# Checks of a bound moved inside a two-layer graph-attention kernel: Gram matrices four at a time, output bias and weight sums later

## The chip, the cores and the metric

The kernel runs on one core of a Trainium2 chip. The metric is the device time of one execution in microseconds (us), and 3038.89 us is the median of three runs of the kernel before (3038.54 to 3039.82). The core has several engines that run side by side, each working through its own list of instructions in order: TensorE (PE in the profile, with its weight loads as PEld) multiplies matrices, VectorE (DVE) and ScalarE (ACT) do elementwise work, GpSimd (POOL) helps with some of it, and SyncE (SP) issues transfers. Results of TensorE land in PSUM, which is used here as eight banks; everything else lives in SBUF.

## The reference, cut to what matters

There are 64 graphs ("batches" here) of 256 nodes with 512 features, and one 256x256 adjacency matrix for all.

```python
# layer 0: one attention head whose scores are a sum of two node terms
h = relu(layernorm(x));  Wh = h @ W
logits = leaky_relu(e_src[:, None] + e_dst[None, :], 0.2)    # e = Wh . a_src, Wh . a_dst
x = x + softmax(where(adj == 0, -inf, logits)) @ Wh
# layer 1: eight heads of 64
h = relu(layernorm(x))
q, k, v = h @ Wq.T + bq, h @ Wk.T + bk, h @ Wv.T + bv
attn = softmax(where(adj == 0, -inf, q @ k.T / 8))           # per head
x = x + (attn @ v) @ Wo.T + bo
```

The kernel computes both softmaxes without taking a maximum out first. That is safe as long as the scores are bounded, and the bound follows from the weights. So the kernel also proves the bound on the chip: for each pair of heads of Wq and Wk it forms a Gram matrix (a 128x128 block of weights times itself, with the parts between the two heads masked away by `diag`), squares it twice, and compares the row sums of absolute values with a limit. It also compares the squared lengths of the vectors `wa` and of the query and key biases, and the sum of squares of Wv. All answers go into a table `ok`; its smallest value per row, `okm`, goes through a last 1x1 matmul (`pok`) into a `flag`. After the main program the flag is read, and a general version of the kernel would run if the bound weren't proven. With the weights at hand it doesn't run. Nothing in the main program waits for the flag.

## The kernel before

**Stages.** The work on a batch g is cut into generators, each of which emits some instructions and yields: `normalize0` (three steps: statistics, activation `h`, node products on DVE with `wa`), `weights0` (edge weights: exponentials on ACT, then maximum, mask and sum on DVE, giving `em` and `esum`), `aggregate0` (matmuls into `pu`, copied to `uT`, then the row sums), `transform0` (matmuls with W into `po`, and the residual read on DVE, L495), `normalize1` (statistics, then `nmr` and the activation `xn`), `transpose1` (transposes into `pt`, `hT`, and sums of its blocks by `combine`), `project_qk` and `project_v` (seven products each, in a form of Strassen's scheme that needs the combined weights of `combine_w`, L161 to L165), `attention` (scores `psc`, exponentials, masks on DVE, values `pav`, row sums), `scale` and `output`.

**Order.** TensorE, VectorE, ScalarE and SyncE run exactly in the order in which the Python code emits instructions: the order is written out by hand. The lists `first`, `second`, `period` and `last` at the end of `bounded()` name a stage and a batch offset; `step(stage, g)` runs one stage up to its next yield. Period i works on batch i in layer 1, on i+1 and i+2 in layer 0, and on the outputs of i-2. The first pass (i = 0) uses `first + second`, after a prologue written out line by line. A matmul that needs a VectorE result emitted just before it therefore waits for all of VectorE's earlier entries too, and everything behind it on TensorE waits with it.

**The side work.** The proof is one more generator, `constants()`. `aside()` runs it up to its next yield. In the kernel before it is called four times in the prologue and then after every step of the first pass, until it is used up. Each of the eight Gram matrices (two weights, four blocks) goes alone through three calls: Gram matmuls (L333) and masking on DVE (L335); first squaring (L338) and a copy on DVE (L340); second squaring (L343) and the absolute row sums on ACT (L345). Then come the table entries (L347 to L363), the squares of Wv in four steps (L372), the reductions (L377 to L382) and the last matmul (L385). The first call also computes the output bias: `bv` times Wo into `pbias` (L307), added to `bo` (L314). GpSimd adds that bias to x, at L519, right after the activation `xn`.

**Buffers.** PSUM tiles come from a pool of eight banks, `bank()`. The copies of the upper right weight quarter, which the combined weights overwrite, come into two buffers with the tag `b12`, which the bias rows (L357) use as well.

Of the kernel before, what the change touches and what calls it, by code (L numbers as in the profile page):

```python
# [9 lines left out]
F32 = mybir.dt.float32  # L10
I32 = mybir.dt.int32
AF = mybir.ActivationFunctionType
# [4 lines left out]
P = 128  # L17
# [11 lines left out]
def kernel(  # L29
# [102 lines left out]
    def bounded():  # L132
# [6 lines left out]
        def bank(shape, name):  # L139
            return ps_mm.tile(shape, F32, tag="mm", name=name)  # L140
# [15 lines left out]
        def quarter_of(src, i, j):  # L156
            return src[i * HD : (i + 1) * HD, j * HD : (j + 1) * HD].rearrange(
                "(c p) e -> p c e", p=P
            )
# [134 lines left out]
            combine_w(wq_sb)  # L294
            combine_w(wk_sb)

        def constants():


            def whole(wt, src, nm):  # L300
                b12 = work.tile([P, DC // 2, HD], F32, tag="b12", name=f"b12_{nm}", bufs=2)
                nc.gpsimd.dma_start(b12, quarter_of(src, 0, 1))
                return ((wt[:, B11], b12), (wt[:, B21], wt[:, B22]))

            pb = bank([P, D], "pbias")
            for c in range(DC):
                nc.tensor.matmul(  # L307
                    pb,
                    cols["bv"][:, c : c + 1].to_broadcast([P, P]),
                    wo_sb[:, c, :],  # L310
                    start=(c == 0),
                    stop=(c == DC - 1),
                )
            nc.vector.tensor_add(bo_b, pb, bo_b)  # L314
            yield

            ok = weights.tile([P, 2 * DC + 5], F32, tag="ok", name="ok")  # L320
            diag = weights.tile([P, P], F32, tag="diag", name="diag")
            nc.vector.memset(diag, 0.0)
            nc.vector.memset(diag[0:DH, 0:DH], 1.0)
            nc.vector.memset(diag[DH:P, DH:P], 1.0)
            rows = weights.tile([P, 2 * DC], F32, tag="rows", name="rows")
            for j in range(2 * DC):
                e = j % DC
                if e == 0:
                    w_q = whole((wq_sb, wk_sb)[j // DC], (wqT, wkT)[j // DC], "qk"[j // DC])
                pg = bank([P, P], f"pgram_{j}")  # L330
                for c in range(DC):
                    wc = w_q[c // 2][e // 2][:, c % 2, (e % 2) * P : (e % 2 + 1) * P]
                    nc.tensor.matmul(pg, wc, wc, start=(c == 0), stop=(c == DC - 1))  # L333
                gm = work.tile([P, P], F32, tag="gram", name=f"gram_{j}", bufs=2)
                nc.vector.tensor_mul(gm, pg, diag)  # L335
                yield
                pg = bank([P, P], f"pgram2_{j}")
                nc.tensor.matmul(pg, gm, gm, start=True, stop=True)  # L338
                gm = work.tile([P, P], F32, tag="gram", name=f"gram2_{j}", bufs=2)
                nc.vector.tensor_copy(gm, pg)  # L340
                yield
                pg = bank([P, P], f"pgram4_{j}")
                nc.tensor.matmul(pg, gm, gm, start=True, stop=True)  # L343
                ab = work.tile([P, P], F32, tag="gabs", name=f"gabs_{j}")
                nc.scalar.activation(ab, pg, AF.Abs, accum_out=rows[:, j : j + 1])  # L345
                yield
            nc.vector.tensor_scalar(ok[:, 0 : 2 * DC], rows, 0.66, None, op0=ALU.is_le)  # L347
            junk = work.tile([P, D], F32, tag="junk", name="junk_b")
            sq = weights.tile([P, 4], F32, tag="sq", name="sq")
            nc.vector.memset(sq, 0.0)  # L350
            for j in range(2):
                nc.vector.scalar_tensor_tensor(
                    junk, wa[j], 1.0, wa[j], op0=ALU.mult, op1=ALU.mult, accum_out=sq[:, j : j + 1]
                )
            for j, src in enumerate((bq, bk)):
                row = work.tile([1, D], F32, tag="b12", name=f"brow_{j}", bufs=2)
                nc.gpsimd.dma_start(row, src.rearrange("(o e) -> o e", o=1))  # L357
                nc.vector.scalar_tensor_tensor(
                    junk[0:1, :], row, 1.0, row, op0=ALU.mult, op1=ALU.mult,
                    accum_out=sq[0:1, 2 + j : 3 + j],  # L360
                )
            nc.vector.tensor_scalar(ok[:, 2 * DC : 2 * DC + 2], sq[:, 0:2], 1.95, None, op0=ALU.is_le)
            nc.vector.tensor_scalar(ok[:, 2 * DC + 2 : 2 * DC + 4], sq[:, 2:4], 1.0, None, op0=ALU.is_le)  # L363
            yield
            big_v = weights.tile([P, 1], F32, tag="big_v", name="big_v")
            wv_q = whole(wv_sb, wvT, "v")
            svs = weights.tile([P, 2 * DC], F32, tag="svs", name="svs")
            for c in range(DC):
                for j in range(2):
                    sqv = work.tile([P, HD], F32, tag="junk", name=f"sqv_{c}_{j}")  # L370
                    wc = wv_q[c // 2][j][:, c % 2, :]
                    nc.vector.scalar_tensor_tensor(  # L372
                        sqv, wc, 1.0, wc, op0=ALU.mult, op1=ALU.mult,
                        accum_out=svs[:, 2 * c + j : 2 * c + j + 1],
                    )
                yield
            nc.vector.tensor_reduce(big_v, svs, AX.X, ALU.add)  # L377
            nc.vector.tensor_scalar(
                ok[:, 2 * DC + 4 : 2 * DC + 5], big_v, 1.0e8, None, op0=ALU.is_le
            )  # L380
            okm = weights.tile([P, 1], F32, tag="okm", name="okm")
            nc.vector.tensor_reduce(okm, ok, AX.X, ALU.min)  # L382
            yield
            pk = bank([1, 1], "pok")
            nc.tensor.matmul(pk, okm, ones[:, 0:1], start=True, stop=True)  # L385
            nc.vector.tensor_scalar(flag, pk, P - 0.5, None, op0=ALU.is_lt)
# [113 lines left out]
        def normalize1(g):  # L500
            xt = xts[g]
            mv = small.tile([P, NT, 2], F32, tag="mv", name=f"mv1_{g}")
            for t in range(NT):
                token_stats(mv[:, t, :], xt[:, t, :], f"1_{g}_{t}", small)
                if t == 0:
                    yield
            rstd = inverse_std(mv, f"1_{g}", small)
            yield
            nmr = small.tile([P, NT], F32, tag="nmr1", name=f"nmr1_{g}")
            nc.vector.scalar_tensor_tensor(  # L510
                nmr, mv[:, :, 0], -1.0, rstd, op0=ALU.mult, op1=ALU.mult
            )
            norms[g] = big.tile([P, NT, D], F32, tag="xn", name=f"xn_{g}")
            for t in range(NT):
                nc.scalar.activation(  # L515
                    norms[g][:, t, :], xt[:, t, :], AF.Identity,
                    bias=nmr[:, t : t + 1], scale=rstd[:, t : t + 1],
                )
                nc.gpsimd.tensor_tensor(xt[:, t, :], xt[:, t, :], bo_b, op=ALU.add)  # L519
            yield  # L520

        def transpose1(g):
# [6 lines left out]
            for t in range(NT):  # L529
# [3 lines left out]
                nc.scalar.activation(hT[:, :, t * P : (t + 1) * P], pt, AF.Relu)  # L533
                yield
            lefts[g] = a, combine(a, ("hs", str(g)))
            yield

        def project_qk(g):
# [168 lines left out]
        def steps(*todo):  # L707
            for stage, g in todo:
                step(stage, g)
# [3 lines left out]
        def aside(n=1):  # L713
            for _ in range(n):
                next(side, END)
# [14 lines left out]
        steps((normalize0, 0), (normalize0, 0))  # L730
        node_weights()
        edge_mask()
        steps((normalize0, 0), (weights0, 0), (normalize0, 1), (weights0, 0))
        steps((aggregate0, 0), (aggregate0, 0))
        prepare_qk()
        steps((aggregate0, 0), (aggregate0, 0), (normalize0, 1), (transform0, 0), (transform0, 0))
        steps((normalize1, 0), (transform0, 0), (transform0, 0), (normalize1, 0))
        aside()
        step(normalize1, 0)
        aside(3)  # L740
        steps((transpose1, 0), (transpose1, 0), (transpose1, 0), (normalize0, 1))
        combine_w(wv_sb)
        first = [
            (load, 3), K, K, (weights0, 1), K, N0, K, (weights0, 1), N0, K, (aggregate0, 1),
            (aggregate0, 1), N0, K, (aggregate0, 1), (aggregate0, 1), W,
        ]
        for i in range(G + 2):
            for stage, ahead in last if i == G else period if i else first + second:
                step(stage, i + ahead if (stage, ahead) not in ((weights0, 1), (aggregate0, 1)) else 1)
                aside()  # L750
        assert next(side, END) is END
        for gen in running.values():
            assert next(gen, END) is END
# [206 lines left out]
```

## Time and profile before

| | |
|---|---|
| median time | 3038.89 us |
| span of the profiled run | 3038.1 us |
| TensorE busy | 2989.2 us, 98% |
| TensorE weight loads busy | 2185.8 us, 72% |
| VectorE busy | 2124.6 us, 70% |
| ScalarE busy | 940.7 us, 31% |
| GpSimd busy | 296.4 us, 10% |
| granted TensorE clock, mean | 0.996 |

"Busy" is the sum of the instructions' durations with overlaps counted once, so a busy TensorE can still be one that runs at half pace. A float32 matmul shows as two records ("passes") in the trace; four matmuls that build one 128x128 Gram matrix are eight passes. In a row of the timeline the first number is the start in us from the span's beginning, the second the duration of the merged group, and the brackets hold the idle time of that engine before it and what ended this idle time.

### The profile page before, as it was taken

Reading aid. Unit: us, or ns where it says so; the run is one execution under the profiler, and the core shown is the slowest. Engines: PE = TensorE matmul, PEld = TensorE weight load, DVE = VectorE, ACT = ScalarE, POOL = GpSimd, SP = SyncE. Lnnn points to the kernel's source line nnn. Section 1 sums busy time; section 2 is a strip of 40 time slices with the busy share of each in tenths; the row PEclk is TensorE's granted clock in tenths of the full one; section 3 lists DMA queues with packets and bytes.
Section 4 is the critical chain, followed back from the end, with each engine's and each line's share of the span. In section 5 each row is a group of like instructions: output and inputs, shape, how many; then the busy total and the mean of one; then the engine's idle time right before and its main releaser. Section 6 shows DMA issues by size and latency. Waiting matters only on the chain. (4 is left out here: it accounts for less than half of the span.)

```text
span 3038.1 us, 45803 instructions
## 1 busy us (share of the span) xinstructions
PE 2989.2 (98%) x18166; PEld 2185.8 (72%) x18166; DVE 2124.6 (70%) x4118; ACT 940.7 (31%) x2003; POOL 296.4 (10%) x279
## 2 busy tenths in 40 slices
PE   6999999999999999999999999999999999999998
PEld 4777777777777777777777777777777777777775
DVE  5767777677677677677776776776776777777764
ACT  2333333333233233333333332332332333333321
POOL 1101101001011011011011010110110110110100
PEclk9999999999999999999999999999999999999999
DMA  3112222122122122122121221221221221222213
GB/s 125 11 35 36 33 38 35 30 41 35 29 39 39 29 39 37 31 39 31 37 36 31 40 36 29 42 35 29 39 39 29 39 32 36 36 32 39 29 23 42
DMA packets 82062, 110.79 MB, mean 36 GB/s; under 512 B 11762, under 2 KB 47602, under 8 KB 81842
## 3 DMA queue, kind: packets, MB, share of 16 engines
q1 hardware_dynamic: 81122, 105.95, 21.8%
q8 instruction: 145, 2.38, 0.3%
q0 software_dynamic: 720, 1.85, 0.2%
q14 instruction: 75, 0.61, 0.1%
HBM read 40.64 MB, written 33.55 MB: 24 GB/s over the span
## 5 line engine op out<-in xcount | busy, mean ns | idle before, releaser
L478 PE MATMUL po<-wo_sb,aT 128*128 128x512 f32 x1024 | 483.0, 595 | 4.7 <-DVE aT L671 4.7
L478 PE MATMUL po<-w_sb,uT 128*128 128x512 f32 x1024 | 471.0, 593 | 0.0
L611 DVE TENSOR_TENSOR ex<-ex,maskT 128x512 f32<-128x512 f32 x512 | 396.1, 814 | 7.3 <-ACT ex L606 1.4
L221 PEld LDWEIGHTS pqk<-hs,wq_sb 128*128 128x128 f32 x2048 | 265.1, 193 | 89.4 <-issue 89.4
L106 POOL TENSOR_TENSOR rstd<-ve,minus_half 128x2 f32<-128x2 f32 x128 | 89.6, 700 | 2382.4 <-DVE ve L104 2382.4
L606 ACT ACTIVATE ex<-psc 128x512 f32<-128x512 f32 x512 | 264.4, 602 | 125.6 <-PE psc L598 125.6
L478 PEld LDWEIGHTS po<-w_sb,uT 128*128 128x128 f32 x1024 | 180.1, 191 | 154.0 <-issue 154.0
L221 PE MATMUL pqk<-hs,wk_sb 128*128 128x128 f32 x2048 | 272.1, 276 | 0.0
L221 PE MATMUL pqk<-hs,wq_sb 128*128 128x128 f32 x2048 | 271.7, 276 | 0.0
L478 PEld LDWEIGHTS po<-wo_sb,aT 128*128 128x128 f32 x1024 | 175.9, 192 | 132.6 <-issue 129.8
L495 DVE SCALAR_TENSOR_TENSOR x<-po,rs,x 128x512 f32<-128x512 f32 x128 | 96.1, 750 | 240.8 <-PE po L478 240.8
L598 PE MATMUL psc<-qk 64*128 64x256 f32 x2048 | 255.7, 389 | 0.0
L221 PEld LDWEIGHTS pqk<-hT,wq_sb 128*128 128x128 f32 x1536 | 196.1, 191 | 80.2 <-issue 59.3
L623 PE MATMUL pav<-ex,v 128*64 128x256 f32 x2048 | 250.9, 386 | 2.8 <-DVE ex L611 2.3
L212 PE MATMUL pv<-wv_sb,hs 128*128 128x256 f32 x1024 | 253.2, 380 | 0.0
L221 PEld LDWEIGHTS pqk<-hs,wk_sb 128*128 128x128 f32 x2048 | 251.0, 193 | 0.0
L453 PE MATMUL pu<-em,h 128*128 128x256 f32 x1024 | 245.0, 383 | 3.7 <-DVE em L438 3.7
L613 DVE TENSOR_TENSOR sm<-ex 128x512 f32<-128x512 f32 x256 | 235.9, 922 | 8.9
L403 ACT ACTIVATE h<-x,nmr,rstd 128x512 f32<-128x512 f32 x128 | 97.2, 806 | 467.6 <-DVE nmr L396 467.6
L598 PEld LDWEIGHTS psc<-qk 64*128 64x128 f32 x2048 | 187.3, 186 | 68.4 <-issue 26.2
L519 POOL TENSOR_TENSOR x<-x,bo_b 128x512 f32<-128x512 f32 x128 | 197.7, 1563 | 255.5 <-ACT xn L515 255.5
L631 ACT COPY aT<-pav 128x512 f32<-128x512 f32 x128 | 75.1, 587 | 472.4 <-PE pav L623 459.9
(147 smaller groups left out, 3932.2 us busy)
## 6 DMA issues: line engine op xcount, KB each, us to landing
x<-in_x_dram SPq DMA_DIRECT2D x64, 512.0 KB, 5.4
rb<-rc SPq DMA_DIRECT2D x512, 64.0 KB, 4.7
out_dram<-x SPq DMA_DIRECT2D x128, 256.0 KB, 2.0
w_sb<-in_L_gnn_W_dram SPq DMA_DIRECT2D x1, 1024.0 KB, 8.5
wq_sb<-in_L_gnn_Wq_dram SPq DMA_DIRECT2D x4, 256.0 KB, 16.1
wk_sb<-in_L_gnn_Wk_dram SPq DMA_DIRECT2D x4, 256.0 KB, 12.5
wo_sb<-in_L_gnn_Wo_dram SPq DMA_DIRECT2D x1, 1024.0 KB, 8.5
wv_sb<-in_L_gnn_Wv_dram SPq DMA_DIRECT2D x4, 256.0 KB, 8.5
```

Source lines behind the costliest of these rows:

```text
L212: nc.tensor.matmul(dst[:, 0:HD], left[:, c, :], wt[:, slot, c, :], start=c == 0, stop=c == 1)
L221: nc.tensor.matmul(dst[:, at : at + P], wt[:, slot, c, e * P : (e + 1) * P], left[:, c, :], start=c == 0, stop=c == 1,)
L403: nc.scalar.activation(h[:, t, :], xt[:, t, :], AF.Relu, bias=nmr[:, t : t + 1], scale=rstd[:, t : t + 1])
L453: nc.tensor.matmul(pu[:, d, :], h[:, m, (dp + d) * P : (dp + d + 1) * P], em[:, m, :], start=(m == 0), stop=(m == NC - 1),)
L478: nc.tensor.matmul(dst, left(c, t), w_t[:, c, :], start=(c == 0), stop=(c == DC - 1))
L495: nc.vector.scalar_tensor_tensor(xt[:, t, :], po, rs[:, t : t + 1], xt[:, t, :], op0=ALU.mult, op1=ALU.add)
L519: nc.gpsimd.tensor_tensor(xt[:, t, :], xt[:, t, :], bo_b, op=ALU.add)
L598: nc.tensor.matmul(psc[r][:, m, :], qk[rows, 2 + e % 2, m * P : (m + 1) * P], qk[rows, e % 2, :], start=True, stop=True,)
L606: nc.scalar.activation(ex[:, r, :, :], psc[r], AF.Exp, scale=SCALE)
L611: nc.vector.tensor_mul(ex[:, r, :, :], ex[:, r, :, :], maskT)
L613: nc.vector.tensor_add(sm, ex[:, :, 0, :], ex[:, :, 1, :])
L623: nc.tensor.matmul(pav[r * DH : (r + 1) * DH, i, :], v[j][:, m, at : at + DH], pair[i][:, r, m, :], start=(m == 0), stop=(m == NC - 1),)
```

## The change

The change rearranges the proof and what stands beside it; what is computed stays the same.

- The Gram matrices go four at a time, one weight after the other, in six calls of `aside()`: 16 matmuls into four banks; four maskings on DVE; four squarings; four copies, now on ACT instead of DVE; four second squarings; four absolute row sums on ACT. A result is read one call after it was computed. The buffers for masked matrices grow from two to four.
- The first batch of four Gram matrices is emitted in the prologue after the first step of batch 0's `weights0`, where TensorE waits for that stage's second step. Its masking and first squaring follow batch 0's transform, the copies follow `normalize1`.
- In the first pass (i = 0) there is no further `aside()`. From period 1 on it is called after every second step.
- The output bias is a function of its own, emitted after those copies, and GpSimd's addition of it to x is emitted at the end of `transpose1` instead of in `normalize1`.
- The third step of batch 1's `normalize0` moves from the prologue to behind the first product of `project_qk`, and the combination of the value weights from the prologue to the beginning of `second`.

```diff
-        def constants():
+        def output_bias():
...
             nc.vector.tensor_add(bo_b, pb, bo_b)
-            yield
+
+        def constants():
...
-            for j in range(2 * DC):
-                e = j % DC
-                if e == 0:
-                    w_q = whole((wq_sb, wk_sb)[j // DC], (wqT, wkT)[j // DC], "qk"[j // DC])
-                pg = bank([P, P], f"pgram_{j}")
-                for c in range(DC):
-                    wc = w_q[c // 2][e // 2][:, c % 2, (e % 2) * P : (e % 2 + 1) * P]
-                    nc.tensor.matmul(pg, wc, wc, start=(c == 0), stop=(c == DC - 1))
-                gm = work.tile([P, P], F32, tag="gram", name=f"gram_{j}", bufs=2)
-                nc.vector.tensor_mul(gm, pg, diag)
-                yield
-                pg = bank([P, P], f"pgram2_{j}")
-                nc.tensor.matmul(pg, gm, gm, start=True, stop=True)
-                gm = work.tile([P, P], F32, tag="gram", name=f"gram2_{j}", bufs=2)
-                nc.vector.tensor_copy(gm, pg)
-                yield
-                pg = bank([P, P], f"pgram4_{j}")
-                nc.tensor.matmul(pg, gm, gm, start=True, stop=True)
-                ab = work.tile([P, P], F32, tag="gabs", name=f"gabs_{j}")
-                nc.scalar.activation(ab, pg, AF.Abs, accum_out=rows[:, j : j + 1])
-                yield
+            for n in range(2):
+                w_q = whole((wq_sb, wk_sb)[n], (wqT, wkT)[n], "qk"[n])
+                pgs = [bank([P, P], f"pgram_{n}_{e}") for e in range(DC)]
+                for e in range(DC):
+                    for c in range(DC):
+                        wc = w_q[c // 2][e // 2][:, c % 2, (e % 2) * P : (e % 2 + 1) * P]
+                        nc.tensor.matmul(pgs[e], wc, wc, start=(c == 0), stop=(c == DC - 1))
+                yield
+                gms = [
+                    work.tile([P, P], F32, tag="gram", name=f"gram_{n}_{e}", bufs=DC) for e in range(DC)
+                ]
+                for e in range(DC):
+                    nc.vector.tensor_mul(gms[e], pgs[e], diag)
+                yield
+                pgs = [bank([P, P], f"pgram2_{n}_{e}") for e in range(DC)]
+                for e in range(DC):
+                    nc.tensor.matmul(pgs[e], gms[e], gms[e], start=True, stop=True)
+                yield
...
+                for e in range(DC):
+                    nc.scalar.copy(gms[e], pgs[e])
+                yield
+                pgs = [bank([P, P], f"pgram4_{n}_{e}") for e in range(DC)]
+                for e in range(DC):
+                    nc.tensor.matmul(pgs[e], gms[e], gms[e], start=True, stop=True)
+                yield
+                for e in range(DC):
+                    j = n * DC + e
+                    ab = work.tile([P, P], F32, tag="gabs", name=f"gabs_{j}")
+                    nc.scalar.activation(ab, pgs[e], AF.Abs, accum_out=rows[:, j : j + 1])
                 yield
...
-                nc.gpsimd.tensor_tensor(xt[:, t, :], xt[:, t, :], bo_b, op=ALU.add)
...
             lefts[g] = a, combine(a, ("hs", str(g)))
+            for t in range(NT):
+                nc.gpsimd.tensor_tensor(xts[g][:, t, :], xts[g][:, t, :], bo_b, op=ALU.add)
             yield
...
-        steps((normalize0, 0), (weights0, 0), (normalize0, 1), (weights0, 0))
-        steps((aggregate0, 0), (aggregate0, 0))
+        steps((normalize0, 0), (weights0, 0))
+        aside()
+        steps((normalize0, 1), (weights0, 0), (aggregate0, 0), (aggregate0, 0))
         prepare_qk()
         steps((aggregate0, 0), (aggregate0, 0), (normalize0, 1), (transform0, 0), (transform0, 0))
         steps((normalize1, 0), (transform0, 0), (transform0, 0), (normalize1, 0))
+        aside(2)
+        step(normalize1, 0)
         aside()
-        step(normalize1, 0)
-        aside(3)
-        steps((transpose1, 0), (transpose1, 0), (transpose1, 0), (normalize0, 1))
-        combine_w(wv_sb)
+        output_bias()
+        steps((transpose1, 0), (transpose1, 0), (transpose1, 0))
         first = [
-            (load, 3), K, K, (weights0, 1), K, N0, K, (weights0, 1), N0, K, (aggregate0, 1),
-            (aggregate0, 1), N0, K, (aggregate0, 1), (aggregate0, 1), W,
+            (load, 3), K, (normalize0, 1), K, (weights0, 1), K, N0, K, (weights0, 1), N0, K,
+            (aggregate0, 1), (aggregate0, 1), N0, K, (aggregate0, 1), (aggregate0, 1), W,
         ]
         for i in range(G + 2):
-            for stage, ahead in last if i == G else period if i else first + second:
-                step(stage, i + ahead if (stage, ahead) not in ((weights0, 1), (aggregate0, 1)) else 1)
-                aside()
+            for n, (stage, ahead) in enumerate(last if i == G else period if i else first + second):
+                g = i + ahead
+                if i == 0 and ahead == 1 and stage in (normalize0, weights0, aggregate0):
+                    g = 1
+                if i == 0 and n == len(first):
+                    combine_w(wv_sb)
+                step(stage, g)
+                if i and n % 2:
+                    aside()
```

More of the change, by code (lines that the diff above doesn't have):

```diff
@@ L295, in prepare_qk @@
             combine_w(wk_sb)
-        def constants():
[L300 to L303, printed above, removed]
+        def output_bias():
             pb = bank([P, D], "pbias")
@@ L314, in constants, with whole @@
             nc.vector.tensor_add(bo_b, pb, bo_b)
-            yield
+        def constants():
+            def whole(wt, src, nm):
+                b12 = work.tile([P, DC // 2, HD], F32, tag="b12", name=f"b12_{nm}", bufs=2)
+                nc.gpsimd.dma_start(b12, quarter_of(src, 0, 1))
+                return ((wt[:, B11], b12), (wt[:, B21], wt[:, B22]))
             ok = weights.tile([P, 2 * DC + 5], F32, tag="ok", name="ok")
@@ new lines, in constants @@
+            for n in range(2):
[5 more added lines that the diff above has]
+                        nc.tensor.matmul(pgs[e], wc, wc, start=(c == 0), stop=(c == DC - 1))
+                yield
+                gms = [
[3 more added lines that the diff above has]
+                    nc.vector.tensor_mul(gms[e], pgs[e], diag)
+                yield
+                pgs = [bank([P, P], f"pgram2_{n}_{e}") for e in range(DC)]
+                for e in range(DC):
+                    nc.tensor.matmul(pgs[e], gms[e], gms[e], start=True, stop=True)
+                yield
+                gms = [
+                    work.tile([P, P], F32, tag="gram", name=f"gram2_{n}_{e}", bufs=DC)
+                    for e in range(DC)
+                ]
+                for e in range(DC):
[9 more added lines that the diff above has]
+                    nc.scalar.activation(ab, pgs[e], AF.Abs, accum_out=rows[:, j : j + 1])
```

## The prediction

> **What bounds the kernel now.** I read busy time by stretch first. Columns: stretch in us, its length, busy us and instruction count of TensorE (PE), its weight loads, VectorE (DVE), ScalarE (ACT) and GpSimd (POOL), granted clock, DMA share, GB/s.
>
> ```profile
> 0.00:45.90 45.90, 25.42 (x86) 16.08 (x87) 25.67 (x71) 11.24 (x19) 12.28 (x25) 1.00 0.63 206
> 45.90:92.70 46.80, 37.41 (x230) 31.55 (x228) 25.93 (x70) 10.37 (x34) 1.94 (x4) 0.89 0.00 1
> 92.70:115.60 22.90, 16.95 (x91) 13.73 (x90) 17.30 (x49) 6.23 (x11) 4.33 (x4) 0.85 0.05 13
> 115.60:154.90 39.30, 39.30 (x268) 30.75 (x266) 30.17 (x60) 14.61 (x31) 4.49 (x4) 1.00 0.22 28
> 200.00:3000.00 2800.00, 2799.48 (x17125) 2048.95 (x17122) 1981.19 (x3793) 880.42 (x1871) 268.83 (x239) 1.00 0.22 34
> ```
>
> From 115.6 us on PE never rests: 2799.48 of 2800 us. There a removed PE pass shortens the run by its whole length and an added one lengthens it. All slack lies in the first 115.6 us, where PE is busy 79.8 us and its clock is cut twice (0.89, 0.85). The cuts are 45.9 (first projection of batch 0), 92.7 and 115.6 (batch 0's two score steps); the fourth stretch is period 1 up to the same place for batch 1.
>
> Then the waits of PE up to 150 us (total, times, longest):
>
> ```profile
> PE pwa L268 <- DVE junk_a L261: 13.7, 4, 10.7
> PE pgram L338 <- DVE gram L335: 7.5, 5, 5.4
> PE pok L385 <- DVE okm L382: 5.9, 1, 5.9
> PE pu L453 <- DVE em L438: 3.7, 1, 3.7
> PE pgram L343 <- DVE gram L340: 2.6, 3, 1.5
> ```
>
> 16.0 us of these belong to the bound's proof (pgram, pok), which nothing else needs until the end. Last, PE in order of time (start, duration; in brackets idle before and releaser); the four parts are separate looks:
>
> ```profile
> 17.55 1.11 PE L280 MATMUL pmask<-ident,adj_f 128*128 128x128 f32 x4 [1.12 <-DVE adj_f L276]
> ...
> 37.61 3.60 PE L307 MATMUL pbias<-wo_sb,bv_c 128*128 128x512 f32 x8
> ...
> 53.24 0.79 PE L338 MATMUL pgram<-gram 128*128 128x128 f32 x2 [5.39 <-DVE gram L335]
> 53.83 1.91 PE L221 MATMUL pqk<-hs,wq_sb 128*128 128x128 f32 x8
> ...
> 100.69 0.19 PE L385 MATMUL pok<-ones,okm 128*1 128x1 f32 x2 [5.95 <-DVE okm L382]
> 100.85 2.05 PE L212 MATMUL pv<-wv_sb,hT 128*128 128x256 f32 x4
> ```
>
> A squaring at 53.24 holds PE 5.39 us, because its masked Gram matrix stands on DVE behind four node products (L410) and the values' combination (L162 to L165). The eight passes behind it take 1.91 us instead of the 1.06 at 45.90: each long idle is paid twice.
>
> **What the skill says.** The Trainium skill, "TensorE: Matmul & The Clock Gate", Part 1, states that the PE clock is halved after about 3.4 us idle and freed after about 3.4 us of work. The trace agrees: half pace after 5.39 and 5.95 us, full pace some 4 us later. The same page, on architectural detail, calls ACT and DVE strict first-in first-out; 53.24 shows what that costs. "SBUF — State Buffer", on SBUF's two sides, states that DVE and GpSimd share a port pair which one of them locks; here the masking product L611 takes 1.18 us each while the bias addition L519 runs (two in 2.36 at 143.83), and 0.64 without it (two in 1.29).
>
> **The change, part by part.** Pitches by the starts of following work: eight 128-wide passes 0.89 us (45.01 to 45.90), so a whole Gram matrix (four matmuls, shown as eight passes) 0.89 and a squaring 0.22; a 256-wide pass 0.21 (eight, 1.70); a 512-wide pass 0.43.
>
> (1) Four Gram matrices at 20.1. PE idles 3.68 us there, waiting for the edge weights, and the weights have landed: wq's quarters by about 20 (issued 2.3 to 4.0, 16.1 to landing), the fourth quarter at 16.9 (7.1+9.8). 32 passes cost 3.6 us at full pace and 7.1 at half. The four passes at 17.55 ran at half pace, so I take some 5.5, to 25.6. The aggregation then starts 1.8 later but warmer: its 16 passes took 6.5 us (23.78 to 30.30), against 3.4 at full pace. It ends between 28.5 and 31.
>
> (2) After the first transform (end T, 37.6 before) the order is: four maskings, four squarings, copies on ACT, then bias. DVE reaches the maskings at T+2.1, behind residual and statistics, and leaves at T+3.3; PE squares until T+3.4, bias until T+6.9, transposes until T+7.8. Projections start near T+8 (before: 45.90, T+8.3). Equal within 0.5; with (1), **-0.4**, from -2.2 to +1.
>
> (3) Projection to first scores. PE work left there: seven products of 16 passes 12.5, sixteen aggregation passes 3.4, sixteen transform passes 6.9, small ones 0.9: 23.7. DVE's queue gives new waits: node products end near K0+4.5 (PE wants them at 3.6), the edge weights near K0+11 (wanted at 9.9). The values' combination, 2.5 on DVE, now stands before the second half and delays only reads with free banks behind them. 23.7+0.7+1.1 = 25.5 instead of 46.8: **-21.3**. A cross-check: 15.3 idle and 5.3 of half pace (three stretches over twice their due) vanish over (3) and (4), and 79 proof passes (8.7) move out, 29.3 less new waits of 2.8.
>
> (4) First to second scores: the weight sums (eight of 0.46) with 1.67 us of DMA wait, and the 5.95 wait, leave. Period 1 does the same work in 14.7 (140.22 to 154.93); I add 1.0 for DVE's lag: 15.7 instead of 22.9: **-7.2**.
>
> (5) Period 1 receives one batch of four Grams (3.6), three batches of four squarings (2.6), and the last product (0.2): **+6.4**, undiminished since PE has no gap. Waits: the last squarings need copies behind the activation h on ACT, **+1.0** (0 to 2). While four banks are held, four turn over for the rest; I count nothing for that, at most 2. Then DVE. Batch 1's residual read frees DVE at 132.8. From there on the old clock it must do: ok, norms and bias rows 3.2 (89.88 to 93.08), weight sums 3.7, their transfer's rest 0.9 (landing 3.6 after the first bias row's read, less 2.7 of work), reductions 0.6, and its own statistics, residual, q/k read, reciprocal and edge weights, 6.6; ends at about 148. The final 1x1 matmul is emitted after the first values' product, which ends at 143.0: PE waits some **5.0** (1.4 if DVE has no lag, since edge weights end only at 143.9; 6 otherwise). Queued behind it are all the values' products. A wait over 3.4 brings half pace for some 3 us: **+1.5** (0 to 2). Sum +13.9.
>
> (6) The bias addition is emitted after the transposes. GpSimd's rows show it released by ACT's xn each time I looked (143.3 to 144.2, 189.5 to 190.4), and the change adds no operand, so it should start at the same moment; from period 2 on, nothing changes: 0.
>
> Sum: -0.4-21.3-7.2+13.9 = -15.0. **3038.9-15.0 = 3023.9 us.**
>
> **Rivals.** *The check is hidden* (25%): PE, slowed by 7 us in period 1, lets DVE catch up, and only the 1.4 remains. For: DVE idles 5.1 us between 130 and 140. Against: I count that idle already. 6.4+1.0+1.4 = 8.8; 3038.9-28.9+8.8 = 3018.8. *DVE becomes the bound* (8%): DVE works 43.2 us in the 69.7 of (3) and (4). Some 11 leave (maskings, copies, ok, weight sums), so 32 must fit into my 41.2. They should; but if DVE's order costs 14 us there, the gain is only that of (1) and a little: 3023.9+14 = 3038. *The repeated period suffers* (7%), the one on the slower side: the bias addition follows the transposes and its lock meets the combination (L170 to L173) and the maskings behind. At 0.3 us in each of 62 periods, 18.6: 3023.9+18.6 = 3042.5. Against: (6), and the period's PE has no DVE wait from 200 to 400 us that a small shift would lengthen. The forecast has 60%.
>
> **How the numbers follow.** Likeliest 3024. The first rival and the best ends of (1) and (5) reach 3014; the worst ends, with banks, reach 3033. Outside lie both bad rivals and a little more, under 2 in 10. Faster by over 0.2% (below 3032.8): 60+25 and 1 more, 0.86; within 0.2%: 0.07; slower: 0.07.
>
> **What would show it.** Right: Gram passes from 20.1; the first scores near 71 and the second near 87; busy PE from there except a wait of 3 to 6 us at the proof's last product, and some 6.4 us of pgram passes in period 1. Wrong: an aggregation that ends after 31; second scores after 95, which would make DVE the bound; period 1 with no wait (first rival) or with many bank waits; a period after 200 us longer than before.

## The result and the profile after

The changed kernel takes 3025.86 us (median of six runs, 3024.34 to 3028.91), beside 3039.36 us for the kernel before in the runs taken with it. The ratio is 0.9956, with a 95% interval from 0.9944 to 0.9969. The forecast was 3023.9 us, with a range from 3014 to 3033.

First the busy time by stretch, with the columns of the prediction's first fence. The cuts are at the same four places of the program: first projection of batch 0, its first and second score step, and the second score step of batch 1.

```profile
0.00:46.70 46.70, 28.48 (x106) 19.67 (x106) 26.06 (x72) 11.03 (x21) 10.52 (x25) 0.96 0.62 203
46.70:73.70 27.00, 24.61 (x152) 19.46 (x152) 20.73 (x47) 8.49 (x22) 3.18 (x3) 1.00 0.00 1
73.70:89.40 15.70, 14.99 (x90) 12.22 (x89) 13.40 (x25) 5.99 (x11) 3.60 (x3) 1.00 0.01 2
89.40:143.80 54.40, 48.91 (x326) 39.13 (x324) 37.12 (x96) 18.10 (x51) 5.66 (x6) 0.94 0.18 25
200.00:3000.00 2800.00, 2797.04 (x17111) 2045.73 (x17114) 1981.00 (x3789) 878.69 (x1867) 269.09 (x239) 1.00 0.22 35
```

The second stretch shrank from 46.8 to 27.0 us and lost its cut in the clock (0.89 before). The fourth grew from 39.3 to 54.4: TensorE executes 58 passes more there, idles 5.5 us, and runs at a mean clock of 0.94. In the last row TensorE is idle for 3.0 us instead of 0.5; the added 2.4 us lie after 2989 us, in the drain at the end of the run, which comes 11 us sooner and so begins before the fixed cut at 3000. In exact starts (first projection 46.76, scores 73.71, 89.40 and 143.83) the account is:

| Stretch | before | after | change | forecast |
|---|---|---|---|---|
| to the first projection | 45.90 | 46.76 | +0.9 | -0.4 |
| to the first scores | 46.85 | 26.95 | -19.9 | -21.3 |
| to the second scores | 22.87 | 15.69 | -7.2 | -7.2 |
| period 1 (to batch 1's second scores) | 39.31 | 54.43 | +15.1 | +13.9 |
| all the rest | 2883.2 | 2883.3 | +0.1 | 0 |

The sum is -11.0, the difference of the two profiled spans (3038.1 and 3027.1). The profiled execution of the changed kernel is the slowest of its six (3028.91); the medians differ by 13.5.

The waits of TensorE in the first 160 us:

```profile
PE pwa L268 <- DVE junk_a L261: 13.9, 4, 10.5
PE pok L400 <- DVE okm L397: 5.5, 1, 5.5
PE pgram L344 <- DVE gram L340: 2.3, 1, 2.3
PE pe L439 <- DVE junk L425: 1.3, 2, 0.8
PE pmask L280 <- DVE adj_f L276: 1.1, 1, 1.1
PE pu L468 <- DVE em L453: 1.0, 1, 1.0
PE pu L468 <- DVE s2v L197: 0.7, 1, 0.7
PE pqk L221 <- DVE hs L171: 0.7, 1, 0.7
```

The proof's waits fell from 16.0 us to 7.8, and what is left is two single waits. The last product's wait of 5.5 us is the old one (5.9) at a new place. TensorE in order of time around them, in three parts:

```profile
20.07 3.62 PE L334 MATMUL pgram<-wq_sb 128*128 128x128 f32 x16
...
26.31 3.62 PE L468 MATMUL pu<-em,h 128*128 128x256 f32 x16
...
39.52 2.05 PE L344 MATMUL pgram<-gram 128*128 128x128 f32 x8 [2.28 <-DVE gram L340]
41.36 4.28 PE L301 MATMUL pbias<-wo_sb,bv_c 128*128 128x512 f32 x8
...
122.31 1.13 PE L212 MATMUL pv<-wv_sb,hT 128*128 128x256 f32 x4
128.93 0.19 PE L400 MATMUL pok<-ones,okm 128*1 128x1 f32 x2 [5.49 <-DVE okm L397]
129.05 2.07 PE L212 MATMUL pv<-wv_sb,hs 128*128 128x256 f32 x4
```

At 20.07 the gap is gone: 32 Gram passes take 6.24 us, more than the 3.7 of the gap, but the 16 aggregation passes behind them take 3.45 instead of 6.5, so that the aggregation ends at 29.8, earlier than before (30.3). At 39.52 there is a new gap, 2.28 us of idle after the transform, the eight squaring passes take 1.84 us where 0.89 is due, and the bias passes behind it are slow (4.11 us from start to start of what follows, against 3.43 before). At 128.93 all of TensorE's work stands behind the last product, which waits for `okm`; the next group takes 1.87 us where 0.86 is due.

### The profile page after: what moved, and what is told of

Read it like the earlier page. It is cut to its first block, busy times and chain, and to the rows that moved or that the text cites. A ratio compares the mean times of both kernels' runs of the same rounds, so it can differ in the third digit from the quotient of the medians.

```text
span 3027.1 us, 45790 instructions
## 1 busy us (share of the span) xinstructions
PE 2987.1 (99%) x18166; PEld 2184.2 (72%) x18166; DVE 2124.1 (70%) x4110; ACT 941.3 (31%) x2011; POOL 296.5 (10%) x279
```

## The experiments

In each, the ratio is to the kernel before, run beside it on the same chip. The median of the kernel before is 3039.36 us beside the changed kernel, 3038.68 beside the next four experiments, 3038.05 beside the three after them and the one without a proof, and 3038.14 beside the two others. So a difference between two kernels of different groups is uncertain by about 1 us, and where it matters I read it in the traces too.

### The last product later

```diff
+            for _ in range(12):
+                yield
             pk = bank([1, 1], "pok")
```

> The changed kernel, with the proof's last 1x1 matmul and the flag emitted twelve calls later, so that it falls into period 2. Theory: the 5.5 us wait for okm and the half pace behind it (16 values' passes in 6.4 us instead of 3.4) leave, 8.8 us in all, and about 1.5 us come back as a wait of the aggregation for the edge weights, which VectorE finishes late: 3026 - 7 = 3019 us. Rival: VectorE's lateness is the real bound and the wait only moves to the next VectorE result: 3024 us or more.

Measured: 3019.33 us, ratio 0.9935 (0.9921 to 0.9948), 6.5 us below the changed kernel (5.9 if each is taken from the kernel before beside it). Period 1 takes 47.82 us (87.07 to 134.89) instead of 54.43, and the product finds its operand ready:

```profile
118.06 2.00 PE L616 MATMUL psc<-qk 64*128 64x256 f32 x16
131.40 0.66 PE L548 MATMUL pt<-ident,xn 128*128 128x128 f32 x4 [0.80 <-DVE s2v L197]
133.45 1.52 PE L641 MATMUL pav<-ex,v 128*64 128x256 f32 x12 [0.33 <-DVE v L206]
134.89 2.00 PE L616 MATMUL psc<-qk 64*128 64x256 f32 x16
144.02 0.19 PE L402 MATMUL pok<-ones,okm 128*1 128x1 f32 x2
```

So the wait was a cost of its own. VectorE's lag does come back, nearly in the size expected (1.1 us for 1.5), but as waits of 0.8 and 0.3 us for the values' sums rather than for the edge weights.

### The same move on the kernel before

The same lines with 24 in place of 12, and nothing else. Here a call comes after every step and there after every second one, so the distance in steps is the same.

> The kernel before with its last 1x1 matmul emitted 24 calls later, nothing else. Theory: VectorE carries the squares of the value weights ahead of the edge weights, so the aggregation waits for em at about 102.8 us where the matmul waited until 100.7; only part of the 5.95 us and the 2.1 us of half pace is won: 3035 to 3037 us. Rival, the matmul's wait is a cost of its own: 3039.4 - 8 = 3031 us.

Measured: 3035.56 us, ratio 0.9990 (0.9984 to 0.9997). Here the wait moved on:

```profile
91.86 2.00 PE L600 MATMUL psc<-qk 64*128 64x256 f32 x16
93.79 1.13 PE L212 MATMUL pv<-wv_sb,hT 128*128 128x256 f32 x4
...
96.48 1.89 PE L212 MATMUL pv<-wv_sb,hs 128*128 128x256 f32 x8
102.65 2.67 PE L455 MATMUL pu<-em,h 128*128 128x256 f32 x8 [4.28 <-DVE em L440]
```

The aggregation reaches the edge weights at 98.2 and gets them after 102.6. In the kernel before VectorE itself was late in this stretch; in the changed one, with the weight sums gone, the longest wait of the same stretch is 0.7. The theory holds: the move is worth 3.1 us alone (3038.68 less 3035.56), about half of what it is worth on top of the change.

### Two of the moves alone

```diff
-        steps((transpose1, 0), (transpose1, 0), (transpose1, 0), (normalize0, 1))
-        combine_w(wv_sb)
+        steps((transpose1, 0), (transpose1, 0), (transpose1, 0))
...
-            (load, 3), K, K, (weights0, 1), K, N0, K, (weights0, 1), N0, K, (aggregate0, 1),
+            (load, 3), K, (normalize0, 1), K, (weights0, 1), K, N0, K, (weights0, 1), N0, K, (aggregate0, 1),
...
+                if i == 0 and n == len(first):
+                    combine_w(wv_sb)
...
```

> The kernel before with two of the change's moves alone: batch 1's node products behind the first product, and the values' combination at the beginning of the second half. The proof stays one Gram matrix at a time in the first pass. Theory: the wait of 5.4 us at the first squaring and its 1.6 us of half pace leave, and 2.5 us of VectorE work come back in the second half, where VectorE is late: 3034 to 3036 us. Rival, the order of these two alone carries most of the gain: 3030 us or less. Second rival: VectorE bounds the first pass whatever the order: 3039 us.

Measured: 3031.91 us, ratio 0.9979 (0.9969 to 0.9988), about half of what the whole change gives, and 2 us better than my expectation. The wait of 5.4 us at the first squaring is gone (the longest at any squaring is now 1.0), and the first scores start at 84.18 instead of 92.75. The second half keeps its wait, now behind 2.2 us of VectorE waiting for the transfer of the value weights' quarter:

```profile
92.67 0.19 PE L385 MATMUL pok<-ones,okm 128*1 128x1 f32 x2 [6.49 <-DVE nmr L510]
```

The other half of the gain isn't taken apart. No run keeps one Gram matrix at a time and only starts the proof later, so it isn't shown what going four at a time, or copying on ScalarE, is worth by itself.

### The proof's first half not in the idle stretches

```diff
         steps((normalize0, 0), (weights0, 0))
-        aside()
...
-        aside(2)
         step(normalize1, 0)
-        aside()
         output_bias()
```

> The changed kernel with the first four Gram matrices, their masking, first squaring and copies moved out of the idle stretches ahead of the first pass; the whole proof now starts in period 1. Theory of the prediction, idle stretches hide them: period 1 gets 4.5 us of TensorE work more and the aggregation of batch 0 runs at half pace again, so 3026 + 5 = 3031 us. Rival, from the trace of the changed kernel: the squarings between transform and bias hold the projections back by about 4 us (2.3 idle, 1.8 of squarings, slow bias passes), so what is hidden at 20 us is paid there again: 3026 to 3027 us.

Measured: 3032.11 us, ratio 0.9978 (0.9968 to 0.9987). The number is the theory's, the reason isn't. The first scores start at 69.40, earlier than in the changed kernel (73.71) and than with the late product (71.38), which is the same program up to there. So the rival is right about the head of the run: what is saved at 20 us is lost again at 39. Period 1 takes 63.3 us, 8.8 more, of which 4.5 are work; the wait for `okm` grew to 10.3.

```profile
69.40 2.00 PE L614 MATMUL psc<-qk 64*128 64x256 f32 x16
...
140.97 0.19 PE L400 MATMUL pok<-ones,okm 128*1 128x1 f32 x2 [10.30 <-DVE okm L397]
```

The next experiment takes that wait away.

### The same with the last product later

The twelve yields before the last product are added to the kernel of the last experiment.

> The kernel with the whole proof in period 1, and its last matmul twelve calls later. If the wait of 10.3 us for okm is what made that kernel slow, it falls from 3032 to about 3022 us: the first scores come 1.7 to 4 us earlier than with the proof's first half ahead, and period 1 has 4.5 us more work. Rival, the 4.5 us and VectorE's lag are the cause and the wait moves on to the next VectorE result: 3028 us or more.

Measured: 3029.24 us, ratio 0.9970 (0.9958 to 0.9981). The rival holds. The wait of 10.3 us becomes two others, the second and third row (of the first, 3.7 is the old gap at 20 us):

```profile
PE pu L470 <- DVE em L455: 4.7, 2, 3.7
PE pt L548 <- DVE s2v L197: 3.8, 1, 3.8
PE pav L641 <- DVE v L206: 1.8, 1, 1.8
```

The table and the weight sums, now four calls later, fall on VectorE among the edge weights, the maskings and the values' sums of period 1, and TensorE waits for them there. In this pair the late product is worth only 2.9 us. Beside the kernel with the late product alone, period 1 takes 58.0 us instead of 47.8; 4.5 of these 10.2 us are work, and the other 5.7 are waits, with the half pace behind them. So where VectorE's share of the proof lies counts for as much here as where the last product lies.

### The bias first

On top of the late last product, the bias matmuls fill the gap after the transform, and the squarings follow them.

```diff
-            nc.vector.tensor_add(bo_b, pb, bo_b)
+            return pb
...
-        aside(2)
+        aside()
+        pb = output_bias()
+        aside()
         step(normalize1, 0)
+        nc.vector.tensor_add(bo_b, pb, bo_b)
         aside()
-        output_bias()
```

> The changed kernel with the late last matmul, and in the gap after batch 0's transform the bias matmuls first, then the squarings; the bias is added on VectorE after nmr. Theory: TensorE's 2.3 us of idle there is filled by bias passes, the squarings find their maskings done, and the clock stays up; the projections start 3 to 4 us earlier: 3019.3 - 3.5 = 3016 us. Rival: the projections are held by xn, the transposes and hT on ScalarE, which the order of these matmuls does not move: 3019 us.

Measured: 3016.92 us, ratio 0.9932 (0.9919 to 0.9946). No gap is left between transform and projection except 0.5 us for hT:

```profile
28.44 7.11 PE L495 MATMUL po<-w_sb,uT 128*128 128x512 f32 x16
35.39 3.60 PE L301 MATMUL pbias<-wo_sb,bv_c 128*128 128x512 f32 x8
38.82 1.05 PE L344 MATMUL pgram<-gram 128*128 128x128 f32 x8
39.71 1.05 PE L548 MATMUL pt<-ident,xn 128*128 128x128 f32 x8
41.25 1.16 PE L221 MATMUL pqk<-hT,wq_sb 128*128 128x128 f32 x8 [0.49 <-ACT hT L549]
```

From the transform's start to the first projection it takes 12.8 us, against 15.1 in the kernel with the late product alone (29.35 to 44.42) and 16.6 in the changed kernel's profile (30.13 to 46.76). The gain is 2.4 us of medians (1.8 if each is taken from the kernel before beside it), less than the 3.5 expected.

### VectorE's share spread over three periods

Eight yields before the table, four after each pair of weight sums, three before the last product, on top of the bias first.

> The kernel with the bias first, and VectorE's part of the proof (table, weight sums, reductions) spread over periods 1 to 3 with the last matmul behind it. Theory: the small waits left in period 1 (0.8 and 0.3 us on values' sums) vanish and nothing else changes: 1 us less than the kernel with the bias first, 3015 us. Rival: VectorE's 9 us in period 1 cost TensorE nothing once the last matmul is late: the same time.

Measured: 3022.10 us, ratio 0.9944 (0.9930 to 0.9957): 5.2 us slower, against both theories. In the profiles 1.8 us lie in the head (first scores at 69.14 instead of 67.35), 3.3 in period 1 (51.24 instead of 47.91) and 1.1 in period 2. The head is the same program in both, and its difference comes mostly from a later end of half pace at 20 us; only the 4.4 us of the two periods can be the edit's. The table now stands in VectorE's queue between the values' sums:

```profile
126.16 0.41 DVE L201 TENSOR_TENSOR v<-s2v,pv 128x256 f32<-128x256 f32 x1
126.49 0.17 DVE L364 TENSOR_SCALAR ok<-rows 128x8 f32<-128x8 f32 x1
...
129.69 0.41 DVE L203 TENSOR_TENSOR v<-v,pv 128x256 f32<-128x256 f32 x1
```

and TensorE pays for it at once, in wait and in pace (the last 12 passes of a group of 16 take 2.75 us to the next start, where the whole group is due in 1.9):

```profile
128.64 0.65 PE L644 MATMUL pav<-ex,v 128*64 128x256 f32 x4
133.31 2.83 PE L644 MATMUL pav<-ex,v 128*64 128x256 f32 x12 [4.01 <-DVE v L206]
```

The sum that TensorE waits for, L206, stands on VectorE behind the table, 3.2 us, and also behind the first weight sums, which wait 1.7 us for their transfer. Spreading by count was my mistake: it moved this work out of the slack stretch into the full one.

### Only the weight sums, one period later

On top of the bias first, 22 yields after the table, so that the sums meet the same slack stretch one period on.

> The kernel with the bias first, and only the weight sums and what follows moved by 22 calls, from the slack stretch of period 1 (between the transform and the scores) to the same stretch of period 2. Theory: VectorE's slack lies in that stretch, some 5 us per period; table and sums together overfill it in period 1 and cost 2.2 us there (batch 1's two score steps are 16.9 us apart instead of 14.7), while each alone fits: 3016.9 - 2.2 = 3014.7 us, and no wait of TensorE for VectorE in periods 1 and 2. Rival: as in the spread kernel, VectorE's work costs where it lands: 3017 us or more.

Measured: 3014.79 us, ratio 0.9921 (0.9908 to 0.9935). Period 1 then has no idle:

```profile
84.30:130.00 45.70, 45.70 (x324) 37.09 (x322) 33.98 (x76) 17.95 (x51) 5.81 (x6) 1.00 0.22 30
130.00:176.60 46.60, 46.43 (x284) 33.83 (x282) 36.22 (x83) 14.59 (x31) 4.41 (x4) 1.00 0.22 35
```

45.7 us is 6.4 above the 39.3 of the kernel before: the work of four Gram matrices and twelve squarings alone. The theory holds (3014.7); of the expectation one thing failed: period 2 keeps a wait of 0.17 us for a values' sum. The profile's first scores start at 68.65, 1.3 us later than in that of the bias first, so the gain shows in period 1: 45.7 instead of 47.9 us.

### No proof at all

`constants()` isn't run and the flag is set to zero, on top of the bias first: Gram matrices, table and weight sums are left out.

> The kernel with the bias first, with the proof left out and the flag set to zero: no Gram matrices, no table, no weight sums. It gives the price of the proof that is left. Theory: 6.4 us of TensorE work and 1.1 us of waits in period 1 leave, and ahead of it the gain of the four Gram matrices at 20 us (6.2 us of passes) is cancelled by the aggregation that runs at half pace again, but the squarings' 0.9 us leave: 3016 - 8.5 = 3007.5 us. Rival: part of it hides even in period 1: 3011 us or more.

Measured: 3006.58 us, ratio 0.9895 (0.9880 to 0.9911). Period 1 is back at its old length, with TensorE full:

```profile
84.10:123.40 39.30, 39.30 (x268) 30.75 (x266) 30.18 (x60) 14.59 (x31) 4.50 (x4) 1.00 0.23 28
```

Its first scores start at 68.50, no earlier than in kernels that run four Gram matrices and four squarings ahead of them (67.35, 68.65 and 69.14). The aggregation without Gram passes before it takes 5.3 us at the old gap, with them 3.45. So these Gram matrices are free, within the 1.8 us by which profiles of the same head differ. The theory holds (3007.5). The proof costs 18 to 19 us in the changed kernel (3025.86 less 3006.58, or 1.3 less from the kernels before beside them; part of it the place of the bias) and 8.2 with the sums one period later.

### TensorE warmed

```diff
...
+            warm(26)
             for j in range(2):
                 pa = bank([P, D], f"pwa_{j}")
                 for c in range(DC):
+                    if j == 0 and c:
+                        warm(2)
...
             nc.scalar.copy(maskT, pm)
+            warm(2)
```

> The same kernel with matmuls of the identity, whose result nobody reads, in TensorE's idle time before 20 us (26 at the start, two between the transposes of wa). Theory: the Gram passes at 20 us begin at half pace in every run so far[...]; warmed, all 32 take 3.4 us, the first scores move forward by 1 to 2.5 us, and the runs of one kernel lie closer together: 3013 us. Rival: the sparse work between 10 and 20 us lets the clock fall again, or the edge weights on VectorE set the start of the aggregation at about 24: 3014.7 us.

Measured: 3013.74 us (3012.32 to 3014.03), ratio 0.9918 (0.9905 to 0.9932), the fastest version. The theory isn't borne out: the first 16 Gram passes take 3.41 us again, half pace, and the next 16 take 1.79.

```profile
19.42 3.58 PE L343 MATMUL pgram<-wq_sb 128*128 128x128 f32 x16
```

They start 0.3 to 0.7 us earlier than in the other profiles with Gram passes there (19.72 to 20.16), but the first scores, at 67.36, stand where the unwarmed bias-first profile has them (67.35). Whether the last microsecond comes from the warming or from an earlier end of half pace by chance isn't settled; with 1.05 us between the medians and ranges that overlap (3013.47 to 3015.12 unwarmed), I would not claim it.

## Why the prediction was right, step by step

**The direction and the size** came from one reading: TensorE is full from 115.6 us on, so only the head can give, and what moves into a period is paid in full. The table of stretches bears it out. Within it, three terms missed by 1.2 to 1.4 us each, all to the same side, so that the profile shows a gain of 11.0 us where 15.0 were forecast. That the medians, with 13.5, come nearer is in part luck: the profiled execution is the slowest of six, and no trace of a faster one shows which term was smaller there. The remaining periods close to 0.1 us over 2883 us, which rules out the rival of a longer period. GpSimd's bias addition starts where it did, released by xn, the first row before and the second after:

```profile
190.40 3.10 POOL L519 TENSOR_TENSOR x<-x,bo_b 128x512 f32<-128x512 f32 x2 [4.04 <-ACT xn L515]
...
179.30 3.10 POOL L551 TENSOR_TENSOR x<-x,bo_b 128x512 f32<-128x512 f32 x2 [4.04 <-ACT xn L530]
```

**(1)** The Grams ran at half pace for about 26 of 32 passes, 6.24 us instead of 5.5; the aggregation ended at 29.8, inside the bounds given.

**(2)** was the first miss: projections at 46.76 instead of 45.5. The gap of 2.3 us itself was foreseen (squarings that end at T+3.4). What wasn't is that TensorE leaves it at half pace: 0.95 us too much for the eight squaring passes and 0.68 for the bias. In the profile with the late last product the same program left the same gap at full pace and the projections started at 44.42:

```profile
38.74 1.13 PE L344 MATMUL pgram<-gram 128*128 128x128 f32 x8 [2.28 <-DVE gram L340]
```

So the mean of the two is near the forecast, by chance of the two profiles. The bias-first run shows that the order was worth more than I thought: I priced the new sequence against the old one and did not see the gap as something to fill.

**(3)** 26.95 instead of 25.5. The waits for node products (0.6) and edge weights (1.0) came as foreseen (0.7 and 1.1); a third one (0.7, for hs) did not. By the starts of the passes the three cost some 3.1 us, more than the 2.3 of the brackets, since the passes beside a wait are stretched too (the eight behind the wait for hs take 1.00 us instead of 0.89); with the 23.7 us of work this makes nearly all of the 26.95. In the first batch, and only there, (6) is wrong: the bias comes later than xn, so GpSimd adds it at 46.49 to 49.2 instead of 42.93 to 45.4, and VectorE's second sum of `combine`, L171, takes 1.38 us beside it instead of 0.42:

```profile
46.49 2.68 POOL L551 TENSOR_TENSOR x<-x,bo_b 128x512 f32<-128x512 f32 x2 [6.50 <-issue]
48.08 1.38 DVE L171 TENSOR_TENSOR hs<-hs,hT 128x256 f32<-128x256 f32 x1
```

It fits the port pair that DVE and GpSimd share by the Trainium skill, "SBUF — State Buffer", on SBUF's two sides: a VectorE instruction with two inputs in SBUF contends with a GpSimd one that reads SBUF. With the bias first the addition ends earlier, L171 takes 0.43 us and that wait is gone.

**(4)** 15.69 against 15.7. The prediction's own cross-check of (3) and (4), 29.3 less 2.8, comes to 26.5 and not to the 28.5 that it stands beside; the two measure 27.1 together. Had the sum been finished, it would have pointed at the miss in (3).

**(5)** The work is 6.4, as the kernel with the later sums shows. The copies' wait, put at 1.0, did not occur: the last squarings start at 103.97, right behind a product. The wait for `okm` was put at 5.0 and measured 5.5. The half pace behind it was put at 1.5 and cost 3.0 (16 passes from 129.05 to 135.47, 6.4 us where 3.4 are due): that is the term of this sum that was mis-sized most. By the pitches (0.43 and 0.21 us) about 14 of the 16 passes ran at half pace, an estimate of 6 us where the prediction took 3. In the trace before, 100.85 to 105.5 had shown a loss of 2.1 for the same thing, and it would have been the better price.

**The rivals.** That the check hides (3018.8) did not happen by itself; it happens when the product is emitted later, at 3019.3. DVE as the bound was wrong for the head, but inside period 1 its share is not free. The two pairs in which little else moved show it: with the spread share periods 1 and 2 grew by 4.4 us, and with the sums one period later period 1 shrank by 2.2. In the kernels with the whole proof in the period TensorE's work moved too, so the part of VectorE there is argued from the waits.

## What to carry to other kernels

Work that nothing waits for still blocks an in-order engine if one of its instructions stands there before its operand is ready: emit such an instruction well behind its operand. Here 24 steps, about half a period, were enough in both kernels, but in the kernel before the next instruction that needed VectorE then waited in its place, and the move brought 3.1 us only. For a second engine, look not at its mean load but at the stretch: here VectorE gives the table's 3 us away free between a batch's transform and its scores (period 1 of the kernel with the later sums has no idle), and with the table and the first sums behind the scores period 1 is 5.5 us longer (51.24 against 45.71). When idle time is filled, check whether the fill opens a new gap behind it; independent work belongs into the gap, and dependent work behind that.

## What was not expected of the hardware

The start-up depends on more than the program. Three profiles with the same program up to the squarings took 6.24, 5.65 and 4.90 us for the same 32 Gram passes at 20 us (changed kernel, late product, bias first), according to whether half pace ended after about 26, 20 or 13 passes; the third was followed by an aggregation at 24.62 instead of 26.31. The idle of 2.28 us after the transform led to half pace in the first of the three (squarings 1.84 us) and not in the second (0.96). The Trainium skill, "TensorE: Matmul & The Clock Gate", Part 1, describes a free-running window of about 3.4 us that decides the clock. That would explain why the same program meets half pace at different points.

It does not settle how much idle is too much. The prediction took a wait of over 3.4 us as the limit, from the same part of that page, and two waits of the trace before agreed; but in that trace there was a third case, with a longest idle of 1.50 us:

```profile
67.00 0.49 PE L343 MATMUL pgram<-gram 128*128 128x128 f32 x2 [1.50 <-DVE gram L340]
67.32 1.86 PE L221 MATMUL pqk<-hs,wq_sb 128*128 128x128 f32 x8
68.97 1.92 PE L221 MATMUL pqk<-hs,wk_sb 128*128 128x128 f32 x8
70.68 1.11 PE L333 MATMUL pgram<-wk_sb 128*128 128x128 f32 x8
```

These 16 passes take 3.36 us where 1.79 are due. Together with the 2.28 us above it says that shorter gaps can cost the pace, and the measurements decide here; the limit itself stays open.

The start-up may also be why the six runs of the changed kernel spread over 4.6 us; but the kernel before spreads over 1.3 us in six runs and over 4.5 in 35 others (3036.04 to 3040.52), so that cause is argued, not shown. The clock in the table of stretches doesn't show all of this: 20 to 26 us has 1.00 granted in the changed kernel while its passes run at half pace, 0.213 us each instead of 0.112.
